# A graph layer on one core: batches of four steps, gathers tied to one put, 384-byte rows, and a changed readiness test

## The chip, the cores and the metric

The kernel runs on one core of one Trainium2 chip. The metric is device time in microseconds (us) of one execution. Three runs of the kernel before gave 18110.78, 18131.4 and 18134.8 us; their median is 18131.4 us. A further execution was recorded by the hardware profiler, and all rows of a profile come from it.

The engines are called as the profile calls them: PE is TensorE (its weight loads, which overlap the matmuls, are PEld), DVE is VectorE, ACT is ScalarE, POOL is GpSimd, and SP is SyncE, which issues most of the DMAs. L641 is line 641 of the kernel.

## The reference

A pre-norm graph layer over 100,000 nodes with 64 channels and 3,300,000 edges, sorted by the node that they end in (`dst`). In numpy terms:

```
h   = relu((x - mean(x)) / sqrt(var(x) + 1e-5))          # per node
y_e = concat(h[dst_e], h[src_e] - h[dst_e]) @ W.T + b    # per edge
s_v = sum of y_e over the edges with dst_e == v
out = x + where(cnt > 0, s / max(cnt, 1), 0)             # cnt: edges per node
```

The part of `y` that depends on `dst` is the same for all edges of a node, so only `h[src] @ W2.T`, 64 numbers a node, has to be summed over edges. The rest is one row a node.

## The kernel before, in words

**First stage.** In 28 iterations over the nodes, the kernel normalizes `x`, transposes it (`turned_of`), multiplies with the weights (`product`), and evicts the product in four parts (`evict`): the node's own part plus `x` plus bias goes to `hb` in float32 (`own`), and the part to be summed (`z`) is split into three bfloat16 numbers, high, middle and low (`first_part`, `second_part`, `third_part`), which together carry float32 precision. They are written to a table `h3` in HBM, one row a node: 3 x 64 numbers and two columns of ones, 388 bytes. The ones make each sum of rows bring its count of edges along. An order by hand (`turn`) fixes the sequence of instructions on each engine, in software-pipelined form: a new iteration is centred while the one before (`mid`) is transposed and multiplied and the one before that (`old`) is split.

**Two ways for the edges.** The sorted edges are cut into 256 windows of 8160 edges, which end in rows 0 to about 63,300, and a rest of 338 chunks of 28 x 128 edges.

- *Chunks.* For each 128 edges POOL issues an indirect DMA that gathers rows of `h3` (`chunks`, L641, 9464 of them) into one of 65 buffers `nb`; a burst of 28 matmuls (L606) against one-hot matrices (`hot_of`) sums a chunk by destination. ACT evicts it (L611), DVE adds the three parts, and SP adds it to its place in HBM (`addition`). `stored[1]` counts the chunks so written.
- *Windows.* First the edges of each window are sorted by source (DVE, with bitonic steps, L710 to L712). Then come the passes: 5 groups, each with one eighty-block share of the table held in SBUF (`tabs`), over 64 sets of four windows, 40 steps to a set. A step has a *pick* (`pick`, L1279: four matmuls that select rows of the table with one-hots `gh`, copied to `gs` by ACT at L1285) and a *put* (`put`, `by_quarters`, L1292: 16 matmuls on a quarter of the array's rows each, which add the picked rows to their destinations with one-hots `dh`). DVE makes the one-hots (`one_hots`, L1257 for `gh`, the helper `one_hot`, L553, for `dh` and for the chunks), in four parts for five steps. The four sums of a set fill four PSUM banks (`total`) and are evicted at its end (L1322, then DVE at L1326 and on). In the last group the sums are final, and SP writes them to HBM; `stored[0]` counts the windows.

**The order of the work in the passes.** `passes` runs over batches of three steps (`BATCH`; the first batch of a set has four): DVE's one-hots of later steps, at a set's start one burst of a chunk, the picks of the next batch, then the puts of this one. The picks use three PSUM banks in turn (`rings`); the eighth bank holds `pairs`, a copy of the ramp `upto` that L553 compares with.

The gathers are spread over the batches by `gathers`: each batch of steps adds its nominal time to `owed`, and for each 1270 ns owed one gather is issued, about 1.9 a batch. A gather is held back by a semaphore (`gated`): it waits for a mark, one of the picks or puts of the batch `BEHIND` = 6 back. The marks list has a batch's picks first and then its puts, and the gathers of a batch take marks spread evenly over the list (`at[i * len(at) // n]`).

**The results.** `results` makes the output in 98 blocks of 1024 rows: it loads two halves of the sums and `hb`, adds, divides by the count and adds again on DVE (L242 to L250), and stores. In the last three groups the passes call it once in two batches (`go_on`); what is left runs after the passes. The blocks are tried in an order that has the 35 blocks that only chunks reach first and then the window blocks from row 0 up. `ready` tells from the counts `stored` whether all that a block needs has been written:

```python
        left, now, before = list(order), None, []
        while left or now:
            before.append(tuple(stored))
            r = next((r for r in left if ready(r, before.pop(0) if len(before) > 2 else (0, 0))), None)
```

The counts grow as the instructions are written out, so this choice is made when the program is built. A result takes five calls: one that starts the loads, two that put DVE's work in place, one that waits and one that starts the store.

Of the kernel before, what the change touches and what calls it, by code (L numbers as in the profile page):

```python
# [13 lines left out]
F32 = mybir.dt.float32  # L14
# [20 lines left out]
NBUF = 65  # L35
# [4 lines left out]
BATCH = 3  # L40
# [8 lines left out]
BEHIND = 6  # L49
# [59 lines left out]
def gnn_preln(ctx: ExitStack, tc, x, src_w, dst_w, src_p, dst_p, src_a, dst_a, wT, b, out, V, E):  # L109
# [51 lines left out]
    h3 = dram.tile([RT, CT], BF16, name="h3")  # L161
# [67 lines left out]
    def results(pool, order, after, start):  # L229
# [27 lines left out]
        while left or now:  # L257
            before.append(tuple(stored))
            r = next((r for r in left if ready(r, before.pop(0) if len(before) > 2 else (0, 0))), None)
            coming = None  # L260
            if r is not None:
                left.remove(r)
                coming = load(r)
            yield
            if now:
                yield from finish(*now)
            else:
                yield
            now = coming
# [8 lines left out]
    with tc.tile_pool(name="pre", bufs=2) as pre, tc.tile_pool(name="small", bufs=4) as small, \  # L278
# [21 lines left out]
        blank = pre.tile([P, CT], BF16, name="blank", bufs=1)  # L300
# [118 lines left out]
        def first_part(i):  # L419

            own, z = owns_z[i]
            parts = split[i] = pre.tile([P, T, CT], BF16, name="parts", bufs=3)
            turn(nc.gpsimd.memset(parts[:, :, C3:], 1.0))
            turn(nc.scalar.copy(parts[:, :, :C], z))
            turn(nc.gpsimd.tensor_tensor(z, z, parts[:, :, :C], ALU.subtract))
# [17 lines left out]
        for i in range(-1, NT1 + 1):  # L443
# [8 lines left out]
            if has(old):  # L452
                evict(old, 3)
            if has(mid):
                turned_of(mid, 0)
            if has(old):
                first_part(old)
# [30 lines left out]
    with tc.tile_pool(name="rows", bufs=6) as rows, \  # L488
# [3 lines left out]
        pairs = rows_ps.tile([P, CH // 2], I32, name="pairs", bufs=1)  # L492
        nc.vector.tensor_copy(pairs, upto.bitcast(I32))
        upto = pairs.bitcast(I16)
# [29 lines left out]
        count = [0, 0]  # L524
        rings = [rows_ps.tile([P, 512], F32, name="ring0", bufs=1)]
# [34 lines left out]
        def chunks(first, n, dynamic=None):  # L560
# [68 lines left out]
            for e in range(n * J):  # L629
# [8 lines left out]
                if not in_passes[0]:  # L638
                    burst(20)
                nbs[e] = rows.tile([P, CT], BF16, name="nb", bufs=NBUF)  # L640
                last[POOL] = gated(nc.gpsimd.indirect_dma_start(  # L641
                    out=nbs[e], out_offset=None, in_=h3,
# [566 lines left out]
        def passes():  # L1209
# [5 lines left out]
            def fetch(t):  # L1215
# [17 lines left out]
                if final and s == 2 * SL + 1:  # L1233
                    owns[v] = load.tile([P, QW, NT, CT], BF16, name="own", bufs=1)
                    for r in range(QW):
                        at = number(wb_r[0:1, ds(u * QW + r, 1)], SP, V - CH)
                        sync(owns[v][:, r], h3[ds(at, CH)].rearrange("(b p) f -> p b f", p=P))
                if final and s == 2 * SL + 4:
                    beyond[v] = rows_x = load.tile([P, 1, CT], BF16, name="rows_x", bufs=2)
                    last[POOL] = nc.gpsimd.indirect_dma_start(  # L1240
                        out=rows_x[:, 0], out_offset=None, in_=h3,
                        in_offset=bass.IndirectOffsetOnAxis(ap=spilled[0][:, u:u + 1], axis=0))
# [25 lines left out]
            def pick(t):  # L1268
# [6 lines left out]
                gs[t] = hots.tile([P, 2, CE], BF16, name="gs", bufs=2 * BATCH + 1)  # L1275
# [85 lines left out]
            for of, ahead in zip(batches, batches[1:] + [()]):  # L1361
                for q in of:
                    fetch(q + AHEAD)
                    if q % SL < 2 * NT:
                        one_hots(q - q % SL + SL, q % SL)
# [15 lines left out]
        def load_table(k, g):  # L1381

            for i in range(2):
                sync(tabs[k][:, i],
# [3 lines left out]
        with tc.tile_pool(name="few", bufs=1) as few:  # L1388
# [3 lines left out]
            def gathers(ns):  # L1392
# [4 lines left out]
                for i in range(n):  # L1397
                    if at:
                        gate[0] = at[i * len(at) // n]
# [15 lines left out]
            with ExitStack() as held:  # L1415
                with tc.tile_pool(name="keys", bufs=1) as big, tc.tile_pool(name="counts", bufs=1) as counts:
# [6 lines left out]
                    rings.extend(g_ps.tile([P, 512], F32, name=f"ring{i}") for i in (1, 2))  # L1423
# [4 lines left out]
                with tc.tile_pool(name="load", bufs=3) as load, tc.tile_pool(name="hots", bufs=3) as hots, \  # L1428
                        tc.tile_pool(name="a_ps", bufs=1, space=PSUM) as a_ps:
                    for k in range(NBT):  # L1430
                        tabs.append(load.tile([P, 2, SL * NT, CT], BF16, name=f"tab{k}", bufs=1))
# [52 lines left out]
    with tc.tile_pool(name="any", bufs=2) as edge, tc.tile_pool(name="any_c", bufs=1) as one, \  # L1484
# [5 lines left out]
        with tc.For_i(0, n_slow, 1) as c:  # L1490
# [7 lines left out]
            nb = edge.tile([P, JA, CT], BF16, name="nb")  # L1498
            for j in range(JA):
                nc.gpsimd.indirect_dma_start(  # L1500
                    out=nb[:, j], out_offset=None, in_=h3,
# [85 lines left out]
```

## Time and profile before

| what | value |
|---|---|
| runs, median | 18131.4 us |
| the profiled execution's own time | 18148.31 us |
| its span in the trace | 18146.6 us |
| PE busy | 13049.6 us (72%) |
| DVE busy | 10919.6 us (60%) |
| POOL busy | 9972.4 us (55%) |
| ACT busy | 7142.4 us (39%) |
| passes, from and to | 2769 to 17867 us |
| what runs after the passes | 280 us |

The profiled execution is some 17 us above the median of the runs. A share of busy time is an average over the stages: in the first some 450 us the product of `x` is made, then the sort of the windows runs to about 2350 us with DVE in the lead, then the windows' borders are placed, and the passes take the most of the span. Rows of a timeline give start and length in us, the engine, line and operation, the count of instructions that the row joins, and in brackets the idle time of the engine before it with what ended it. "issue" is time in which the engine waited for nothing that the profile shows.

### The profile page before, as it was taken

How to read it: one execution, taken by the hardware profiler on the slowest of the kernel's cores; microseconds unless marked ns; L12 is line 12 of the kernel's file. 1: busy time of each engine (PE TensorE's matmuls, PEld its weight loads, DVE VectorE, ACT ScalarE, POOL GpSimd, SP SyncE). 2: the span in 40 equal slices, each digit the busy share in tenths (PEclk: the TensorE clock that was granted, in tenths of full speed). 3: DMA queues.
4: the chain of work that ended last, by engine and by line, in shares of the span. 5: the costliest groups of instructions: out<-in, count | busy, mean ns of one | idle time of the engine just before them, and what ended most of it. 6: DMA issues, size and time to landing. Idle time of an engine off the chain costs nothing. (4 is left out here: it accounts for less than half of the span.)

```text
span 18146.6 us, 617591 instructions
## 1 busy us (share of the span) xinstructions
PE 13049.6 (72%) x264285; PEld 10030.0 (55%) x264285; DVE 10919.6 (60%) x17830; ACT 7142.4 (39%) x15829; POOL 9972.4 (55%) x9922
## 2 busy tenths in 40 slices
PE   6111107888888888888888888888888888888883
PEld 4010105666666666666666666666666666666662
DVE  6788886666666654555555555555555555555555
ACT  5233353434444343344444444443444344444441
POOL 6666645555555555555555555555555555555551
PEclk8555558999999998999999999999999999999996
DMA  5511124333333433333444433343334345444446
GB/s 199 198 36 37 37 60 114 101 98 98 100 100 100 116 102 89 95 102 103 120 131 109 104 103 103 103 122 103 103 104 103 102 110 124 115 115 114 115 115 192
DMA packets 1630181, 1948.47 MB, mean 107 GB/s; under 512 B 998138, under 2 KB 1001794, under 8 KB 1622466
## 3 DMA queue, kind: packets, MB, share of 16 engines
q1 hardware_dynamic: 1307332, 1415.01, 27.2%
q0 software_dynamic: 316480, 493.19, 12.8%
q8 instruction: 2066, 33.85, 0.8%
q14 instruction: 703, 5.76, 0.1%
q10 hardware_dynamic: 3600, 0.67, 0.0%
HBM read 1626.63 MB, written 281.14 MB: 105 GB/s over the span
## 5 line engine op out<-in xcount | busy, mean ns | idle before, releaser
L641 POOL DMA_INDIRECT nb<-h,si x9464 | 9342.2, 987 | 7297.4 <-PE ring L1279 3969.3
L1285 ACT CAST gs<-ring 128x386 bf16<-128x386 f32 x12800 | 5386.9, 491 | 8015.4 <-PE ring L1279 7411.6
L1292 PE MATMUL total<-gs,dh 32*128 32x193 bf16 x200704 | 6803.3, 249 | 2029.7 <-issue 1784.1
L1292 PEld LDWEIGHTS <-dh 32*128 32x128 bf16 x200704 | 4578.6, 94 | 4096.0 <-issue 3902.7
L553 DVE TENSOR_TENSOR dh<-dt,pairs 128x1536 bf16<-128x1536 int16 (+1 forms) x5120 | 3998.2, 816 | 4257.0 <-PE total L1292 2461.5
L1279 PE MATMUL ring<-tab,gh 128*128 128x193 bf16 x50176 | 5278.3, 252 | 572.0 <-issue 206.7
L1279 PEld LDWEIGHTS <-gh 128*128 128x128 bf16 x51200 | 4228.9, 99 | 1303.9 <-issue 850.4
L1257 DVE TENSOR_SCALAR gh<-srs,who_f 128x1280 bf16<-128x1280 int16 x5120 | 2698.0, 566 | 2072.9 <-PE ring L1279 1843.6
L606 PE MATMUL ring<-nb,hot 128*128 128x193 bf16 x9464 | 1016.4, 271 | 1830.2 <-issue 865.0
L606 PEld LDWEIGHTS <-hot 128*128 128x128 bf16 x9464 | 886.4, 107 | 1941.3 <-issue 1022.3
L710 ACT COPY tmp<-keys 128x1536 f32<-128x1536 f32 (+26 forms) x525 | 647.6, 1243 | 895.4 <-DVE keys L712 434.0
L711 DVE TENSOR_TENSOR keys<-tmp,keys 128x1536 f32<-128x1536 f32 (+26 forms) x525 | 749.6, 1459 | 333.5 <-issue 185.5
L553 DVE TENSOR_TENSOR hot<-near,pairs 128x896 bf16<-128x896 int16 x1352 | 780.6, 611 | 0.0
L712 DVE TENSOR_TENSOR keys<-tmp,keys 128x1536 f32<-128x1536 f32 (+26 forms) x525 | 750.2, 1455 | 0.9
L1322 ACT COPY whole<-total 128x386 f32<-128x386 f32 x1280 | 522.6, 496 | 468.4 <-PE total L1292 344.9
L1326 DVE TENSOR_TENSOR whole<-whole 128x512 f32<-128x512 f32 x640 | 439.7, 687 | 29.6 <-ACT whole L1322 13.0
L611 ACT COPY stage<-ring 128x193 f32<-128x193 f32 x338 | 109.1, 323 | 727.9 <-remote 418.3
L1165 DVE COPY_PREDICATED kw<-bits,kw 128x504 int32<-128x504 int32 (+11 forms) x637 | 328.4, 516 | 17.1
L396 PE MATMUL o_ps<-weights,hT 128*128 128x256 f32 x784 | 246.5, 466 | 120.9 <-ACT hT L388 84.7
L1140 POOL DMA_INDIRECT kw<-ksort,at x196 | 195.0, 995 | 245.2 <-DVE bits L1161 75.1
L396 PEld LDWEIGHTS o_ps<-weights,hT 128*128 128x128 f32 x784 | 173.0, 233 | 170.8 <-ACT hT L388 91.5
L616 DVE TENSOR_REDUCE sums<-stage 128x64 f32<-128x192 f32 x338 | 124.0, 367 | 180.5 <-ACT stage L611 109.2
(196 smaller groups left out, 3128.8 us busy)
## 6 DMA issues: line engine op xcount, KB each, us to landing
srs<-sr_d SPq DMA_DIRECT2D x2560, 320.0 KB
nb<-h,si POOLq DMA_INDIRECT x9464
part_d<-wsums SPq DMA_DIRECT2D x256, 260.0 KB
prev<-part_d SPq DMA_DIRECT2D x256, 260.0 KB
acc<-zeros SPq DMA_DIRECT2D x56, 910.0 KB
dt<-dt_d SPq DMA_DIRECT2D x2560, 10.0 KB
tab<-h SPq DMA_DIRECT2D x80, 485.0 KB
h<-parts SPq DMA_DIRECT2D x28, 1358.0 KB
```

Of the source, the lines that this page charges most:

```text
L553: return nc.vector.tensor_tensor(out.rearrange("p k (a d) -> p k a d", d=D), numbers[:, :, None].to_broadcast(shape), upto[:shape[0], :n]. ...
L606: in_turn(nc.tensor.matmul(ps[:, :CE], lhsT=hots_of[q, j // JH][:, j % JH], rhs=nbs.pop(q * J + j)[:, :CE], start=j == 0, stop=j == J - 1))
L641: last[POOL] = gated(nc.gpsimd.indirect_dma_start(out=nbs[e], out_offset=None, in_=h3, in_offset=bass.IndirectOffsetOnAxis(ap=of[q][1][:, ...
L710: last[ACT] = nc.scalar.copy(tmp, lo)
L711: nc.vector.tensor_tensor(lo, tmp, hi, ALU.min)
L712: last[DVE] = nc.vector.tensor_tensor(hi, tmp, hi, ALU.max)
L1257: nc.vector.tensor_scalar(ghots[v, k][:, part].rearrange("p c i s -> p (c i s)"), srs[v, k].rearrange("p c i s -> p (c i s)"), who_f[:, pa ...
L1279: mm = nc.tensor.matmul(gp[:, i], lhsT=ghots[v, k][:, b, c, i], rhs=of[:, :CE], start=b == 0, stop=b == NT - 1)
L1285: in_turn(nc.scalar.copy(gs[t], gp))
L1292: mm = nc.tensor.matmul(total[:, r, b * CE:b * CE + CE], lhsT=dh[at, i, b * P:b * P + P], rhs=rows_of[at, i, :CE], start=begin and i == 0 ...
L1322: in_turn(nc.scalar.copy(whole[:, r], total[:, r, :NT * CE]))
L1326: todo.append(lambda i=i: nc.vector.tensor_add(summed[:, :, :C], summed[:, :, :C], whole[:, :, i * C:i * C + C]))
```

## The change

The change has five parts.

1. Batches of four steps in place of three (`BATCH`), ten to a set. `gs` has eight buffers, the rings get a fourth PSUM bank, and the copy `pairs` goes away: L553 reads `upto` from SBUF. The four parts of the one-hots are made at steps 0, 1, 3 and 4 of five.
2. All gathers of a batch wait for the same mark, the put ahead of the last one of the batch four back.
3. The rows of `h3` have 384 bytes, without the two columns of ones. The ones are written once into the buffers that the rows are loaded to (`with_ones`): 63 fixed buffers for the gathers, the eight tables, `own` and `rows_x`; the memset of each iteration's `parts` goes away.
4. In the first stage `evict(old, 3)` comes after `turned_of(mid, 0)`.
5. In `results` the counts are taken from `before` once for a call and used for all blocks that are tried.

```diff
-NBUF = 65
+NBUF = 63
-BATCH = 3
+BATCH = 4
+PARTS_AT = 0, 1, 3, 4
-BEHIND = 6
+BEHIND = 4
...
-    h3 = dram.tile([RT, CT], BF16, name="h3")
+    h3 = dram.tile([RT, C3], BF16, name="h3")
...
             before.append(tuple(stored))
-            r = next((r for r in left if ready(r, before.pop(0) if len(before) > 2 else (0, 0))), None)
+            then = before.pop(0) if len(before) > 2 else (0, 0)
+            r = next((r for r in left if ready(r, then)), None)
...
-            parts = split[i] = pre.tile([P, T, CT], BF16, name="parts", bufs=3)
-            turn(nc.gpsimd.memset(parts[:, :, C3:], 1.0))
+            parts = split[i] = pre.tile([P, T, C3], BF16, name="parts", bufs=3)
...
-            if has(old):
-                evict(old, 3)
             if has(mid):
                 turned_of(mid, 0)
             if has(old):
+                evict(old, 3)
                 first_part(old)
...
-        pairs = rows_ps.tile([P, CH // 2], I32, name="pairs", bufs=1)
-        nc.vector.tensor_copy(pairs, upto.bitcast(I32))
-        upto = pairs.bitcast(I16)
...
+        def with_ones(pool, shape, name):
+            rows_of = pool.tile([P, *shape, CT], BF16, name=name, bufs=1)
+            axes = " ".join("abc"[:len(shape)])
+            flat = rows_of.rearrange(f"p {axes} f -> p ({axes}) f") if shape else rows_of[:, None]
+            nc.vector.memset(flat[:, :, C3:], 1.0)
+            return rows_of
+
+        fetched_rows = [with_ones(rows, (), f"nb{i}") for i in range(NBUF)]
...
-                nbs[e] = rows.tile([P, CT], BF16, name="nb", bufs=NBUF)
+                nbs[e] = fetched_rows[e % NBUF]
                 last[POOL] = gated(nc.gpsimd.indirect_dma_start(
-                    out=nbs[e], out_offset=None, in_=h3,
+                    out=nbs[e][:, :C3], out_offset=None, in_=h3,
...
-                gs[t] = hots.tile([P, 2, CE], BF16, name="gs", bufs=2 * BATCH + 1)
+                gs[t] = hots.tile([P, 2, CE], BF16, name="gs", bufs=2 * BATCH)
...
-                    if q % SL < 2 * NT:
-                        one_hots(q - q % SL + SL, q % SL)
+                    if q % SL in PARTS_AT:
+                        one_hots(q - q % SL + SL, PARTS_AT.index(q % SL))
...
                     if at:
-                        gate[0] = at[i * len(at) // n]
+                        gate[0] = at[max(0, len(at) - 2)]
...
-                    rings.extend(g_ps.tile([P, 512], F32, name=f"ring{i}") for i in (1, 2))
+                    rings.extend(g_ps.tile([P, 512], F32, name=f"ring{i}") for i in (1, 2, 3))
...
-                        tabs.append(load.tile([P, 2, SL * NT, CT], BF16, name=f"tab{k}", bufs=1))
+                        tabs.append(with_ones(load, (2, SL * NT), f"tab{k}"))
+                    own_rows = with_ones(load, (QW, NT), "own")
+                    spilled_rows = [with_ones(load, (1,), f"rows_x{i}") for i in range(2)]
```

The loads of the tables, of `own` and of `rows_x` write only the first 192 columns in the same way.

More of the change, by code (lines that the diff above doesn't have):

```diff
@@ L299, in gnn_preln @@
         load_x(T)
-        blank = pre.tile([P, CT], BF16, name="blank", bufs=1)
+        blank = pre.tile([P, C3], BF16, name="blank", bufs=1)
         nc.gpsimd.memset(blank, 0.0)
@@ L1233, in fetch @@
                 if final and s == 2 * SL + 1:
-                    owns[v] = load.tile([P, QW, NT, CT], BF16, name="own", bufs=1)
+                    owns[v] = own_rows
                     for r in range(QW):
                         at = number(wb_r[0:1, ds(u * QW + r, 1)], SP, V - CH)
-                        sync(owns[v][:, r], h3[ds(at, CH)].rearrange("(b p) f -> p b f", p=P))
+                        sync(owns[v][:, r, :, :C3], h3[ds(at, CH)].rearrange("(b p) f -> p b f", p=P))
                 if final and s == 2 * SL + 4:
-                    beyond[v] = rows_x = load.tile([P, 1, CT], BF16, name="rows_x", bufs=2)
+                    beyond[v] = rows_x = spilled_rows[v % 2]
                     last[POOL] = nc.gpsimd.indirect_dma_start(
-                        out=rows_x[:, 0], out_offset=None, in_=h3,
+                        out=rows_x[:, 0, :C3], out_offset=None, in_=h3,
                         in_offset=bass.IndirectOffsetOnAxis(ap=spilled[0][:, u:u + 1], axis=0))
@@ L1383, in load_table @@
             for i in range(2):
-                sync(tabs[k][:, i],
+                sync(tabs[k][:, i, :, :C3],
                                   h3[ds((i * NCB + g * SG + k * SL) * CELL, SL * CELL)].rearrange("(x p) f -> p x f", p=P))
@@ L1498, in gnn_preln @@
             nb = edge.tile([P, JA, CT], BF16, name="nb")
+            nc.vector.memset(nb[:, :, C3:], 1.0)
             for j in range(JA):
                 nc.gpsimd.indirect_dma_start(
-                    out=nb[:, j], out_offset=None, in_=h3,
+                    out=nb[:, j, :C3], out_offset=None, in_=h3,
                     in_offset=bass.IndirectOffsetOnAxis(ap=si[:, j:j + 1], axis=0))
```

## The prediction

> **What bounds the kernel now.** I read the page first (busy shares, the granted clock, the groups), then windows, then timelines of single batches.
>
> ```profile
> span 18146.6 us, 617591 instructions
> PE 13049.6 (72%) x264285; PEld 10030.0 (55%) x264285; DVE 10919.6 (60%) x17830; ACT 7142.4 (39%) x15829; POOL 9972.4 (55%) x9922
> L641 POOL DMA_INDIRECT nb<-h,si x9464 | 9342.2, 987 | 7297.4 <-PE ring L1279 3969.3
> L1292 PE MATMUL total<-gs,dh 32*128 32x193 bf16 x200704 | 6803.3, 249 | 2029.7 <-issue 1784.1
> ```
>
> No engine is full. In the passes TensorE leads, and its largest idle is 1784.1 us in the puts (L1292) where no engine is named as the cause. The windows that follow are two groups of the passes, with the gathers alone counted (columns: length, POOL busy and count, granted clock, DMA share, GB/s):
>
> ```profile
> 9038.00:12014.00 2976.00, 1624.96 (x1641) 0.98 0.42 111
> 14990.00:17867.00 2877.00, 1531.67 (x1541) 0.98 0.48 115
> ```
>
> A group is 64 sets, so the first is 2976 / 64 = 46.5 us a set; the clock is nearly full, and the DMA share is under a half. Now a batch of three steps without any gather, at the very end of the passes:
>
> ```profile
> 17847.11 1.19 PE L1279 MATMUL ring<-tab,gh 128*128 128x193 bf16 x12
> 17848.23 1.19 PE L1292 MATMUL total<-gs,dh 32*128 32x193 bf16 x48
> ```
>
> Picks take 1.12 us, puts as much: 2.24 us a batch. A usual batch holds two gathers, apart:
>
> ```profile
> 12003.86 1.18 PE L1279 MATMUL ring<-tab,gh 128*128 128x193 bf16 x12
> 12004.98 1.53 PE L1292 MATMUL total<-gs,dh 32*128 32x193 bf16 x43
> 12006.95 0.32 PE L1292 MATMUL total<-gs,dh 32*128 32x193 bf16 x5 [0.45 <-issue]
> 12007.21 1.02 PE L1279 MATMUL ring<-tab,gh 128*128 128x193 bf16 x10
> 12003.91 0.94 POOL L641 DMA_INDIRECT nb<-h,si  x1 [0.67 <-PE total L1292]
> 12005.63 1.14 POOL L641 DMA_INDIRECT nb<-h,si  x1 [0.78 <-PE ring L1279]
> ```
>
> It takes 12007.21 − 12003.86 = 3.35 us, 1.1 more. The first gather, started with the picks, let TensorE run on through the picks; the second, started in the puts, is followed by TensorE standing in them. So I read it thus: while a gather is issued, and some tenths after, TensorE gets only so far ahead (here some 40 matmuls), then stands. **The passes are bound by TensorE plus these holds**, the tail by results that come after the passes.
>
> **The change part by part.** All against the profiled execution's span, 18146.6 us.
>
> *Readiness test (the tail).* Rows: the last additions of the results (L250; count, the shortest, median and longest duration in ns, first and last start), asked of the tail, and the last matmul, which waited 272.38 us.
>
> ```profile
> L250 DVE TENSOR_TENSOR ht<-ht,at x63: 691/691/693, 17881.9 to 18133.0; 128x512 f32<-128x512 f32 x63
> 18138.85 0.37 PE L1533 MATMUL f_ps<-ident,fewest 128*1 128x128 f32 x1 [272.38 <-DVE fewest L1531]
> ```
>
> 63 of 98 blocks end after the passes, (18133.0 − 17881.9) / 62 = 4.05 us each. The code says why: in `results` the pop from `before` stands inside the search, so only the first block of `left` meets the true counts; the others meet (0, 0) and are never ready. That first block is one that waits for chunks until near the end, though the window blocks behind it are long ready. With one `then` for all they go in the last group. A result takes five calls, the passes call once in two batches, ten batches a set: one result a set, 64 in the group. A chunk covers 3584 × 100000 / 3.3 million = 108.6 rows, a block of 1024 rows takes 9.4 chunks, and at one burst a set about 7 of the 64 turns go to such blocks. A window block needs 1024 / 247 = 4.1 windows, and 4 windows end per set, so these keep step, two or three sets late. About 54 of 63 leave the tail: −54 × 4.05 = **−219 us**. The last group and the tail by windows (PE, PEld, DVE, ACT, POOL busy):
>
> ```profile
> 14990.00:17867.00 2877.00, 2423.93 (x50220) 1884.12 (x50217) 1590.80 (x2707) 1190.01 (x2871) 1590.18 (x1603) 0.98 0.48 115
> 17867.00:18147.00 280.00, 0.37 (x1) 0.08 (x1) 162.97 (x447) 1.16 (x4) 0.00 (x0) 0.51 0.76 241
> ```
>
> A result costs DVE 162.97 / 63 = 2.6 us. In the last group DVE is 1590.80 of 2877 busy, which covers 54 × 2.6 = 140 us. Uncovered it would cost the 140. On SP's queue each brings three loads and a store among the fetches of `srs` and `dt`, which run ten steps (some 12 us) ahead; the true counts are those of two turns before, so a load seldom waits there for the additions that it reads. A result moves 128 × 8 × (65 + 65 + 64 + 64) × 4 bytes = 1.06 MB, 54 of them 57 MB or 20 GB/s beside the group's 115. Bounds −250 to −80.
>
> *First stage.* ACT's copies in one iteration, and the product's wait in two:
>
> ```profile
> 215.91 0.37 ACT L408 COPY z<-o_ps 128x256 f32<-128x256 f32 x1 [1.67 <-DVE own L406]
> 216.18 0.59 ACT L388 COPY hT<-t_ps 128x512 f32<-128x512 f32 x1
> 216.83 3.68 PE L396 MATMUL o_ps<-weights,hT 128*128 128x256 f32 x8 [2.66 <-ACT hT L388]
> 231.92 0.79 PE L396 MATMUL o_ps<-weights,hT 128*128 128x256 f32 x1 [2.66 <-ACT hT L388]
> ```
>
> Iterations take 231.92 − 216.83 = 15.09 us, and TensorE waits 2.66 in each for the hT copy, which stands on ACT behind the last z copy, itself 1.67 us late. `evict(old, 3)` moved behind the first transposes puts the hT copy ahead, 1.67 us earlier at most. The z copy gets later by 0.59, and `first_part`'s cast and POOL's subtraction with it; these end well ahead of their next use. I take 1.5 × 27 = **−40 us**; bounds −45 to 0.
>
> *Ones once.* 28 memsets leave POOL's side of the first stage (nothing waits); 74 small ones come on DVE, 63 of them in the sort, where DVE is the bound. The nearest row, 128x1 copies with their median of 140 ns:
>
> ```profile
> L618 DVE COPY sums<-stage x338: 132/140/152, 571.6 to 17833.2; 128x1 f32<-128x1 f32 x169
> ```
>
> 63 × 0.14 = **+9 us**, bounds 0 to 10. The 384-byte rows, two buffers fewer, the gate's distance (four batches of four are 16 steps, six of three were 18) and the parts' new places I take at 0: the DMA share is 0.42, and of all waits of TensorE, the bursts' for gathered rows come to little (columns: total, times, longest), which bounds these edits at ±63 us:
>
> ```profile
> PE ring L606 <- DMA nb<-h,si: 63.3, 37, 10.6
> ```
>
> *Four steps a batch.* Inside a run matmuls follow at (1.19 − 0.25) / 11 = 0.085 us; twelve are 1.03, yet the next kind starts after 1.12: 0.09 a switch, 0.18 a batch. (The Trainium skill, "TensorEngine Tiling (Array Packing)", Key Properties, has it that changing the tiling mode drains TensorE first; the trace agrees, with these 0.09 us.) A set of 40 steps had 13 batches and now has 10: 3 × 0.18 × 320 = −173 us; some of it lies under holds, **−160**, bounds −175 to −50.
>
> *The gathers' gate.* Both or all three gathers of a batch now wait for one mark, the put ahead of the last in the batch four back, so they start together, back to back. Behind a waiting gather POOL's queue holds only gathers, and the bursts that want their rows come 28 or more gathers later. Two such cases lie in the old trace by chance; two together:
>
> ```profile
> 16285.89 1.19 PE L1279 MATMUL ring<-tab,gh 128*128 128x193 bf16 x12
> 16289.32 0.85 PE L1279 MATMUL ring<-tab,gh 128*128 128x193 bf16 x8
> 16286.09 0.94 POOL L641 DMA_INDIRECT nb<-h,si  x1 [0.98 <-PE total L1292]
> 16287.33 0.94 POOL L641 DMA_INDIRECT nb<-h,si  x1 [0.30 <-issue]
> ```
>
> 3.43 − 2.24 = 1.2 us held. Three together:
>
> ```profile
> 7641.16 1.19 PE L1279 MATMUL ring<-tab,gh 128*128 128x193 bf16 x12
> 7645.80 0.93 PE L1279 MATMUL ring<-tab,gh 128*128 128x193 bf16 x9
> 7641.18 0.94 POOL L641 DMA_INDIRECT nb<-h,si  x1 [3.03 <-PE total L1292]
> 7643.67 0.94 POOL L641 DMA_INDIRECT nb<-h,si  x1 [0.30 <-issue]
> ```
>
> 4.64 − 2.24 = 2.4 held. A batch of four is 2.24 + 8 × 0.085 = 2.92, and what TensorE runs ahead covers 0.25 to 0.3 more of each hold: 0.95 and 2.1. The group's 1641 gathers over 640 batches are 2.56 a batch: 4.4 batches of a set hold two, 5.6 three: 4.2 + 11.8 = 16.0 us a set, less 1.6 where a burst at the set's start fills the hold: 14.4. Before, 46.5 a set less 13 × 2.24, one step more (0.7) and the burst's 28 matmuls (2.4) leaves 14.3. So **0**. Bounds: if a gather holds only one piece of 0.45, as in the usual batch's row, 2.56 × 10 × 0.45 = 11.5 a set, −2.8 × 320 = −900; if TensorE runs no further ahead than before, 4.4 × 1.2 + 5.6 × 2.4 − 1.6 = 17.1 a set, +2.8, +900. I take 0, as the two rows give it.
>
> *`upto` from SBUF.* L553 read it from PSUM; now both its inputs lie in SBUF. Gathers over L553, and over an operation on SBUF alone (L1257):
>
> ```profile
> 17708.45 1.55 DVE L553 TENSOR_TENSOR dh<-dt,pairs 128x1536 bf16<-128x1536 int16 x2 [0.19 <-PE total L1292]
> 17708.69 0.94 POOL L641 DMA_INDIRECT nb<-h,si  x1 [0.73 <-PE total L1292]
> 17720.25 1.01 DVE L1257 TENSOR_SCALAR gh<-srs,who_f 128x1280 bf16<-128x1280 int16 x2
> 17720.34 1.27 POOL L641 DMA_INDIRECT nb<-h,si  x1 [0.74 <-PE ring L1279]
> ```
>
> 0.94 beside 1.27, up to 0.33 us more. A set has eight such pairs of L553, 1.55 in every 46.5 / 8 = 5.8 us, a quarter of the time, so up to a third of some 8000 gathers (1600 a group) meet it: 0 (no price) to 8000 × 0.33 × 0.33 = 870, as the hold passes it on. Single gathers' length was not passed on (the 1.14 above left 3.35), back-to-back spacing is: I take a sixth, **+150**. (The Trainium skill, "GPSIMD Engine Reference", says that GpSimd shares its SBUF path with VectorE and meets it where VectorE has two SBUF inputs: it speaks against this edit, and the 0.94 beside 1.27 agrees.)
>
> *Fourth ring bank.* It can take some of the picks' wait for casts (columns as above): **−30**, bounds −190 to 0.
>
> ```profile
> PE ring L1279 <- ACT gs L1285: 188.6, 204, 1.9
> ```
>
> Sum: −219 − 40 + 9 − 160 + 0 + 150 − 30 = −290. 18146.6 − 290 = 17,857 for an execution like the profiled one, whose own time is 18148.31. The median of the runs is 18131.4, 17 lower: **17,840 us**.
>
> **The rivals.** *A, slower: the holds drop the clock.* Three windows around a triple (PE, PEld, DVE, ACT, POOL busy; granted clock, DMA share, GB/s):
>
> ```profile
> 10728.00:10731.40 3.40, 2.98 (x84) 2.26 (x72) 3.40 (x8) 1.78 (x4) 2.05 (x3) 1.00 0.39 117
> 10731.40:10734.80 3.40, 2.40 (x26) 1.83 (x27) 0.91 (x2) 0.00 (x1) 2.20 (x2) 0.80 0.40 101
> 10734.80:10738.20 3.40, 3.40 (x64) 2.71 (x62) 2.53 (x4) 1.32 (x4) 2.04 (x2) 0.70 0.22 62
> ```
>
> TensorE issued 26 matmuls in 3.40 us, the clock fell, and the next 3.40 us were full and brought only 64 (84 in 2.98 us at the granted 1.00 before). Usually holds come in pieces of 0.45; in 5.6 triples a set, each lengthened by contention, they gather in one window. It decides where some 5% of batches do so: a window at half clock loses at most 1.7 us, less what a hold would have taken anyway, say 1.3; at one batch in ten that is 320 × 1.3 = +420. With contention at 450 instead of 150, +300: 17,840 + 720 = 18,560, and 18,350 with half the drops. (The Trainium skill, "TensorE: Matmul & The Clock Gate", Part 1, has the clock halve after an idle window; the trace agrees with 0.80 and 0.70.) Against it: the groups keep 0.98 though every usual batch is held 1.1. Price 18,450; chance 0.30, of which 0.26 slower, 0.04 near none.
>
> *B, faster: the hold costs less.* Only one mark a batch is now to be passed on in time, so TensorE may run further past gathers. Triples held 1.9 us instead of 2.1 make 4.2 + 10.6 − 1.6 = 13.2 a set, −1.2 × 320 = −380: 17,460; at the lower bound, −900, 16,940. For it: a gather begun with the picks cost nothing at 12003.91. Against: the triple's 2.4. Chance 0.24.
>
> *C: the readiness test doesn't do what it says*, as when the results can't keep pace: the tail keeps 280 us, 17,840 + 219 = 18,059. For it: one result a set leaves no slack. Chance 0.08.
>
> **How the numbers follow.** Forecast 0.38, A 0.30, B 0.24, C 0.08. Time 17,840, the forecast's. The forecast's own range is 17,700 to 18,000 (tail, switches and contention by half). The whole goes from 17,300, below B's price, to 18,500, above A's; about a third of B and two fifths of A lie outside, 0.2. What can be told from no change is about 0.2%, 18,095 to 18,168. Faster: 0.38 + 0.24 + 0.08 − 0.04 (C or the forecast ending near none) = 0.66; same 0.04 + 0.04 = 0.08; slower 0.26.
>
> **What would show it.** Tail: fewer than 12 of L250 after the passes' end, the tail 60 us or so. First stage: iterations of 13.5 us. Switches: ten batches a set, 2.92 where no gather is. Gate: gathers in twos and threes 1.24 us apart; sets near 46.2 us in the middle groups. Contention: L641's mean above 987 ns, over 1.05. Clock: the middle groups' 0.98 kept; 0.9 or less means A. A middle group over 3100 us would make the prediction wrong on the slow side, under 2800 on the fast side.

## The result, and the profile after

The changed kernel takes 17,977.04 us in the median (17,966.12 to 17,990.65), the kernel before 18,131.47: a ratio of 0.9918 with a 95% interval of 0.99 to 0.9935, or 154 us less. Forecast were 17,840 us, or 291 less. The range held the time and the sign was right; about half of the gain is missing, and the terms of the sum that came out otherwise are larger than that: they partly cancel. Two of the executions behind the numbers further down, one of the kernel before (18,550.45 us) and one of a variant of it (18,532.56 us), ran at a granted clock of 0.72 and 0.69 in place of some 0.89; without them the ratio 0.986 given there is 0.987.

Rows of the changed kernel's page (L647 is the gather that was L641, L1298 the put that was L1292):

```profile
L647 POOL DMA_INDIRECT nb<-h,si x9464 | 10239.9, 1082 | 6605.8 <-PE total L1298 4050.9
L1298 PE MATMUL total<-gs,dh 32*128 32x193 bf16 x200704 | 6518.7, 253 | 2403.1 <-issue 2328.0
```

The gathers' mean rose from 987 to 1082 ns, so they do meet the one-hots that now read SBUF, and the puts' idle time without a named cause rose from 1784.1 to 2328.0 us. The same windows as before, a middle group, the last one and the tail, with the gathers alone counted (length, POOL busy and count, granted clock, DMA share, GB/s):

```profile
8929.00:11928.00 2999.00, 1799.04 (x1642) 0.94 0.41 110
14921.00:17917.00 2996.00, 1690.16 (x1545) 0.92 0.51 128
17917.00:17989.00 72.00, 0.00 (x0) 0.53 0.55 171
```

The tail went from 280 to 72 us. The middle group takes 2999 us in place of 2976, and the last 2996 in place of 2877; the clock in them went from 0.98 to 0.94 and 0.92. The last additions of the results in the tail (count, durations in ns, first and last start), and the first stage with the transition from one iteration's product to the next:

```profile
L251 DVE TENSOR_TENSOR ht<-ht,at x11: 691/691/694, 17931.5 to 17975.8; 128x512 f32<-128x512 f32 x11
214.14 1.99 PE L398 MATMUL o_ps<-weights,hT 128*128 128x256 f32 x8 [0.61 <-ACT hT L390]
226.64 1.99 PE L398 MATMUL o_ps<-weights,hT 128*128 128x256 f32 x8 [0.61 <-ACT hT L390]
```

Eleven results are left in the tail in place of 63. An iteration of the first stage takes 226.64 − 214.14 = 12.50 us in place of 15.09.

What holds TensorE in the passes is seen in two batches of four steps:

```profile
10505.06 1.52 PE L1285 MATMUL ring<-tab,gh 128*128 128x193 bf16 x16
10506.52 0.99 PE L1298 MATMUL total<-gs,dh 32*128 32x193 bf16 x31
10507.96 0.28 PE L1298 MATMUL total<-gs,dh 32*128 32x193 bf16 x4 [0.45 <-issue]
10508.69 0.32 PE L1298 MATMUL total<-gs,dh 32*128 32x193 bf16 x5 [0.45 <-issue]
10509.43 0.71 PE L1298 MATMUL total<-gs,dh 32*128 32x193 bf16 x24 [0.42 <-issue]
10510.08 2.47 PE L1285 MATMUL ring<-tab,gh 128*128 128x193 bf16 x16
10512.49 2.15 PE L1298 MATMUL total<-gs,dh 32*128 32x193 bf16 x64
10505.12 0.94 POOL L647 DMA_INDIRECT nb<-h,si  x1 [0.81 <-PE total L1298]
10506.36 1.11 POOL L647 DMA_INDIRECT nb<-h,si  x1 [0.30 <-issue]
10507.78 1.11 POOL L647 DMA_INDIRECT nb<-h,si  x1 [0.30 <-issue]
```

Three gathers start with the picks at 10505.06 and follow each other; the batch takes 10510.08 − 10505.06 = 5.02 us, 2.10 more than the 2.92 without gathers, and that is the price that was forecast for a triple (three gathers in one batch). The next batch shows the second price: its 16 picks take 10512.49 − 10510.08 = 2.41 us, where the batch ahead took 1.46. That is the half clock: the granted clock is 1.00 over the held batch and 0.57 over these picks, though no pause in the held batch is longer than 0.45 us.

### The profile page after: what moved, and what is told of

It is laid out like the page before. It is cut to its first block, busy times and chain, and to the rows that moved or that the text cites. A ratio compares the mean times of both kernels' runs of the same rounds, so it can differ in the third digit from the quotient of the medians.

```text
span 17988.8 us, 612045 instructions
## 1 busy us (share of the span) xinstructions
PE 12952.3 (72%) x264285; PEld 10417.8 (58%) x264285; DVE 11051.6 (61%) x17903; ACT 7448.8 (41%) x15829; POOL 10887.5 (61%) x9894
## 5 line engine op out<-in xcount | busy, mean ns | idle before, releaser
L647 POOL DMA_INDIRECT nb<-h,si x9464 | 10239.9, 1082 | 6605.8 <-PE total L1298 4050.9
L1291 ACT CAST gs<-ring 128x386 bf16<-128x386 f32 x12800 | 5706.3, 489 | 7489.3 <-PE ring L1285 6205.0
L1298 PE MATMUL total<-gs,dh 32*128 32x193 bf16 x200704 | 6518.7, 253 | 2403.1 <-issue 2328.0
L1298 PEld LDWEIGHTS <-dh 32*128 32x128 bf16 x200704 | 4670.1, 96 | 4078.1 <-issue 3868.4
L559 DVE TENSOR_TENSOR dh<-dt,upto 128x1536 bf16<-128x1536 int16 (+1 forms) x5120 | 4014.7, 822 | 3658.8 <-PE total L1298 2386.3
L1285 PE MATMUL ring<-tab,gh 128*128 128x193 bf16 x50176 | 5398.4, 263 | 397.7 <-ACT stage L617 213.9
L1285 PEld LDWEIGHTS <-gh 128*128 128x128 bf16 x51200 | 4569.0, 103 | 1056.8 <-issue 860.5
L1263 DVE TENSOR_SCALAR gh<-srs,who_f 128x1280 bf16<-128x1280 int16 x5120 | 2747.7, 577 | 2399.4 <-PE ring L1285 2094.6
L559 DVE TENSOR_TENSOR hot<-near,upto 128x896 bf16<-128x896 int16 x1352 | 786.3, 619 | 0.0
L398 PE MATMUL o_ps<-weights,hT 128*128 128x256 f32 x784 | 206.5, 406 | 96.6 <-ACT hT L390 68.6
```

Source lines behind the costliest of these rows:

```text
L559: return nc.vector.tensor_tensor(out.rearrange("p k (a d) -> p k a d", d=D), numbers[:, :, None].to_broadcast(shape), upto[:shape[0], :n]. ...
L647: last[POOL] = gated(nc.gpsimd.indirect_dma_start(out=nbs[e][:, :C3], out_offset=None, in_=h3, in_offset=bass.IndirectOffsetOnAxis(ap=of[q ...
L1263: nc.vector.tensor_scalar(ghots[v, k][:, part].rearrange("p c i s -> p (c i s)"), srs[v, k].rearrange("p c i s -> p (c i s)"), who_f[:, pa ...
L1285: mm = nc.tensor.matmul(gp[:, i], lhsT=ghots[v, k][:, b, c, i], rhs=of[:, :CE], start=b == 0, stop=b == NT - 1)
L1291: in_turn(nc.scalar.copy(gs[t], gp))
L1298: mm = nc.tensor.matmul(total[:, r, b * CE:b * CE + CE], lhsT=dh[at, i, b * P:b * P + P], rhs=rows_of[at, i, :CE], start=begin and i == 0 ...
```

## The experiments

The runs were made in four sittings, A to D, and these differ. In A the kernel before takes 18,125.37 us, close to the 18,131.47 of the result above, whose chip isn't on record; in B it takes 13,787.64, in C 18,378.66 and in D 18,385.77. Each comparison is with the kernel before in the same sitting. The record numbers the chips of the sittings 12, 6, 6 and 11: B and C bear the same number, 25 minutes apart, and the record doesn't say whether that is one chip at two times or two chips. So what differs between the sittings need not be the chip. No trace of the kernel before was kept in A to D; rows of it are those of the profile before.

### One part of the change alone (sitting A)

**The readiness test.**

```diff
-            r = next((r for r in left if ready(r, before.pop(0) if len(before) > 2 else (0, 0))), None)
+            then = before.pop(0) if len(before) > 2 else (0, 0)
+            r = next((r for r in left if ready(r, then)), None)
```

> The kernel before with the readiness test of the change alone. The changed kernel's tail fell from 280 to 72 us, but its last group took 120 us more than before. By the prediction's sum the results cost nothing under the passes: the time falls by the tail alone, about 205 us, and the last group stays at 2877 us. The rival: the results that move into the last group take back time there whatever the gathers do, some 1.5 us a set, about 100 us: the time falls by only 100 to 120 us, and the last group takes some 2975 us. A third reading: the 120 us in the last group are the clock's doing (its share of half speed went from 3% to 15%) and come with back-to-back gathers, not with the results: then the last group here is within 30 us of 2877.

17,912.74 us, ratio 0.9882 (0.9866 to 0.9899): 213 us less. Its last group (PE, PEld, DVE, ACT, POOL busy; clock, DMA share, GB/s):

```profile
14970.00:17844.00 2874.00, 2420.31 (x50211) 1875.86 (x50209) 1711.59 (x3099) 1188.65 (x2869) 1599.56 (x1603) 0.99 0.57 136
```

What runs after the passes takes 59 us. DVE's busy time in the last group rose from 1590.80 to 1711.59 us, and the group stayed at 2874 (2877 before), with the clock at 0.99. The results' work under the passes costs nothing that these runs can tell. The rival that they take back 100 us falls.

**The first stage's order.**

```diff
-            if has(old):
-                evict(old, 3)
             if has(mid):
                 turned_of(mid, 0)
             if has(old):
+                evict(old, 3)
                 first_part(old)
```

> The kernel before with the first stage's order of the change alone (the memsets of ones are kept). In the changed kernel an iteration of the first stage takes 12.50 us in place of 15.09, 70 us in all, where 40 were predicted. If the order alone does it, by the wait of 2.66 us that also let the clock fall in each iteration: 68 to 72 us less. If the rest came with the memsets that left POOL: 40 to 45 us less and iterations of 13.5 us.

18,054.45 us, ratio 0.9958 (0.9941 to 0.9975): 71 us less, all of what the changed kernel gains there. The products of two iterations, and then the first stage by windows (same columns as above), of the kernel before and of this one:

```profile
217.17 1.99 PE L396 MATMUL o_ps<-weights,hT 128*128 128x256 f32 x8 [0.61 <-ACT hT L388]
229.67 1.99 PE L396 MATMUL o_ps<-weights,hT 128*128 128x256 f32 x8 [0.61 <-ACT hT L388]
```

```profile
100.00:400.00 300.00, 210.40 (x833) 159.62 (x831) 208.89 (x198) 174.80 (x236) 216.39 (x79) 0.84 0.58 205
```

```profile
100.00:380.00 280.00, 199.11 (x945) 148.98 (x945) 235.03 (x225) 198.99 (x270) 246.30 (x90) 1.00 0.71 251
```

The order alone makes the iteration 12.50 us. The granted clock goes from 0.84 to 1.00: before, the eight matmuls that followed the wait of 2.66 us took 3.68 us (the row at 216.83), now they take 1.99. So the wait cost 1.7 us behind itself, in slow matmuls. The wait itself fell by 2.66 − 0.61 = 2.05 us, and a new one of 1.32 us ahead of the next eight matmuls took a part back. (The Trainium skill, "TensorE: Matmul & The Clock Gate", section "Why this matters for your kernels", advises no idle gaps over some 3 us between bursts of matmuls, or the clock halves. Here the longest gap of an iteration was 2.66 us and the clock 0.84; with none over 1.32 us it is 1.00.)

**The ramp `upto` from SBUF.**

```diff
-        pairs = rows_ps.tile([P, CH // 2], I32, name="pairs", bufs=1)
-        nc.vector.tensor_copy(pairs, upto.bitcast(I32))
-        upto = pairs.bitcast(I16)
```

> The kernel before with the one-hots' ramp read from SBUF alone (no copy in PSUM, the rings keep three banks). The gathers' mean should rise from 987 to about 1070 ns in each theory. If their length is passed on as the prediction took it, a sixth of the worst case: 100 to 200 us slower. If a lone gather's length does not reach TensorE, since the hold of a lone gather did not depend on its length: within 30 us of before, with the clock at 0.97 or above in the middle groups.

18,092.44 us, ratio 0.998 (0.997 to 0.9989): 33 us less, though the gathers' mean rose to 1125 ns. The page's row of the gathers, and a middle group with them alone:

```profile
L638 POOL DMA_INDIRECT nb<-h,si x9464 | 10644.8, 1125 | 5953.8 <-PE ring L1276 2631.9
9017.00:11988.00 2971.00, 1895.65 (x1641) 0.96 0.45 111
```

POOL's busy time in the group went from 1624.96 to 1895.65 us, the clock from 0.98 to 0.96, and yet the group is 5 us shorter. Longer gathers are not passed on to TensorE here, and a somewhat lower clock alone doesn't make a group longer. The time lies just past the 30 us of the second expectation, on the fast side, and the clock just under its 0.97. Why the kernel gains was not tried.

### The mark undone (sitting A)

```diff
-                        gate[0] = at[max(0, len(at) - 2)]
+                        gate[0] = at[i * len(at) // n]
```

> The changed kernel with the gathers of a batch tied to marks spread over the batch four back, as before, in place of one mark. By the prediction's sum two or three gathers together hold TensorE as long as the same number apart: within 60 us of the changed kernel. By the clock's reading, the long holds of gathers back to back are what lets the clock fall (12% of the middle groups at half speed, 4 to 5% before): spread, the clock goes back to 0.97, and at about 0.56 us a gather a set of ten batches takes 2.92 x 10 + 25.6 x 0.56 + 2.4 = 46.0 us in place of 46.8, some 200 to 280 us less than the changed kernel. The other side: with more gathers started in the puts the holds grow, and the time rises by over 100 us.

17,653.08 us, ratio 0.974 (0.9723 to 0.9756): 324 us less than the changed kernel's 17,977.04, more than any of the expectations named, and faster than both kernels. A middle group and the last one, with the gathers alone:

```profile
8813.00:11758.00 2945.00, 1882.06 (x1642) 0.96 0.44 112
14704.00:17552.00 2848.00, 1791.27 (x1543) 0.97 0.56 135
```

A set of the middle group takes 2945 / 64 = 46.0 us. The clock came back from 0.94 to 0.96. The middle group is 2999 − 2945 = 54 us shorter than in the changed kernel, and the last one 148 us, with the same results in it. The one mark costs some 324 us, and nearly half of that lies in the last group.

### Where gathers hold nothing (sitting B)

Four variants of the changed kernel: the ramp back in PSUM with three banks for the rings; the readiness test undone; and the one mark moved to the first put, and to the first pick.

```diff
+        pairs = rows_ps.tile([P, CH // 2], I32, name="pairs", bufs=1)
+        nc.vector.tensor_copy(pairs, upto.bitcast(I32))
+        upto = pairs.bitcast(I16)
...
-                    rings.extend(g_ps.tile([P, 512], F32, name=f"ring{i}") for i in (1, 2, 3))
+                    rings.extend(g_ps.tile([P, 512], F32, name=f"ring{i}") for i in (1, 2))
```

> The changed kernel with the one-hots' ramp back in PSUM and three banks for the rings. The gathers' mean should fall from 1082 to about 1000 ns. If, with gathers back to back, their length is passed on to TensorE (the prediction's +150, which did not show where gathers are apart: there the ramp in SBUF alone made the kernel 33 us faster): 100 to 250 us faster than the changed kernel, and the half-speed share of the middle groups falls from 12% to 6 to 8%. If it is not passed on here either, the lost bank and the 33 us count: 20 to 80 us slower than the changed kernel.

13,886.03 us, ratio 1.0075 (1.0058 to 1.0092).

```diff
-            then = before.pop(0) if len(before) > 2 else (0, 0)
-            r = next((r for r in left if ready(r, then)), None)
+            r = next((r for r in left if ready(r, before.pop(0) if len(before) > 2 else (0, 0))), None)
```

> The changed kernel without the readiness test. The tail comes back, about 208 us. With the gathers spread, the results in the last group cost nothing (alone on the kernel before they took 2875 us for that group against 2877). If they do cost with gathers back to back, the last group falls from 2996 to about 2900 us and the time rises by only 110 us, to 18,085. If the gate alone sets the last group's time: it stays within 25 us of 2996 and the time is about 18,185.

14,888.99 us, ratio 1.08 (1.0782 to 1.0818).

```diff
-                        gate[0] = at[max(0, len(at) - 2)]
+                        gate[0] = at[max(0, len(at) - 4)]
```

> The changed kernel with all gathers of a batch tied to the first put of the batch four back in place of the put ahead of the last: they still go back to back, some 0.7 us earlier in the batch. If what costs is that they go together, the time stays within 80 us of the changed kernel. If what costs is where in the batch they begin (spread, most begin in the last puts ahead of the picks, and a pair begun there holds TensorE 0.55 us, a pair begun with the picks 0.7 to 1.1): about 200 us faster than the changed kernel.

14,769.57 us, ratio 1.0717 (1.0699 to 1.0735).

```diff
-                        gate[0] = at[max(0, len(at) - 2)]
+                        gate[0] = at[0]
```

> The changed kernel with all gathers of a batch tied to the first pick of the batch four back: back to back, some 0.6 us later against the steps than in the changed kernel. If what costs is that they go together: within 80 us of the changed kernel. If what costs is where in the batch they begin, a pair begun well inside the picks holds TensorE 1.2 to 1.7 us and the time is 150 us or more above the changed kernel.

14,761.65 us, ratio 1.071 (1.0692 to 1.0728).

All four expectations took the holds for granted, and this sitting does not show them. Batches of the last of the four, with gathers running all the time:

```profile
8503.46 1.52 PE L1285 MATMUL ring<-tab,gh 128*128 128x193 bf16 x16
8504.92 1.52 PE L1298 MATMUL total<-gs,dh 32*128 32x193 bf16 x64
8506.37 1.52 PE L1285 MATMUL ring<-tab,gh 128*128 128x193 bf16 x16
8502.75 0.94 POOL L647 DMA_INDIRECT nb<-h,si  x1 [0.30 <-issue]
8503.99 1.16 POOL L647 DMA_INDIRECT nb<-h,si  x1 [0.30 <-issue]
8505.46 0.94 POOL L647 DMA_INDIRECT nb<-h,si  x1 [0.30 <-PE total L1298]
```

The batch takes 2.91 us, the time without gathers. In the whole run the puts stand 21.6 us without a named cause, where the changed kernel's stood 2328.0. POOL has work all the time. A middle group of this kernel, with the gathers alone, and then one of the kernel with the ramp in PSUM:

```profile
7432.00:9801.00 2369.00, 1868.07 (x1631) 0.93 0.54 139
7119.00:9244.00 2125.00, 1617.66 (x1633) 0.99 0.61 155
```

With the 0.30 us of issue ahead of each gather, the gathers fill 1868.07 + 1631 × 0.30 = 2357 of 2369 us, and 1617.66 + 1633 × 0.30 = 2108 of 2125. So POOL is the bound in these groups.

The gathers' length then sets the time, and the place of the mark does not (14,770 beside 14,762): the ramp in SBUF, with the fourth bank, costs 14,762 − 13,886 = 876 us there. That is near the full worst case of the prediction, 870, but not by its reckoning: the gathers of the whole kernel got longer by 10606.5 − 9343.6 = 1263 us, more than the prediction allowed for, and a part of that stayed hidden. The two kernels with another mark differ from the changed kernel in nothing else, so by an estimate the change would be some 7% slower there; the changed kernel itself wasn't run in this sitting.

The readiness test, undone, costs 14,889 less some 14,766 = 123 us there, less than its 213 in sitting A. The traces show where the rest went: with the results in it the last group takes 2483 us (the kernel with the mark at the first pick), without them 2396, 87 us less. With them TensorE waits 284 us in that group for DVE's one-hots, without them 63. So where TensorE isn't held, DVE's work for the results is no longer covered.

### The mark with the ramp in PSUM (sitting C)

> The changed kernel with the one-hots' ramp back in PSUM and three banks for the rings, once more, for a chip on which gathers hold TensorE (the kernel before at 18,130 us). If, with gathers back to back, their length is passed on to TensorE: 100 to 250 us faster than the changed kernel's 17,977, with the half-speed share of the middle groups down from 12% to 6 to 8%. If not, the lost bank and the 33 us of the ramp alone count: 20 to 80 us slower, some 18,030. On a chip where gathers hold nothing (the kernel before at 13,790 us) it should repeat 13,886.

18,524.98 us, ratio 1.0083 (1.0066 to 1.01). The same with spread marks (both edits shown above together):

> The changed kernel with spread marks, the ramp back in PSUM, and three banks for the rings. Where gathers hold TensorE: if the ramp in SBUF costs nothing with gathers apart, 20 to 80 us slower than with spread marks alone (17,653 us), some 17,700; if batches of four steps pass the gathers' length on, 50 to 150 us faster, some 17,550. Where they hold nothing, POOL is the bound and only the gathers' length counts, not their marks: within 100 us of 13,886.

17,741.97 us, ratio 0.9656 (0.964 to 0.9672). These two stand in one sitting and differ in the mark alone: it costs 783 us. A middle group and the last one, with the gathers alone, with the one mark and then spread:

```profile
9138.00:12244.00 3106.00, 1595.95 (x1643) 0.93 0.41 106
15344.00:18446.00 3102.00, 1509.10 (x1545) 0.94 0.51 124
```

```profile
8886.00:11843.00 2957.00, 1633.44 (x1642) 0.98 0.44 112
14790.00:17664.00 2874.00, 1535.32 (x1543) 0.99 0.55 134
```

With the one mark the last group, which has some 100 gathers fewer, is as long as the middle one; spread, it is 83 us shorter. Three gathers in a batch and the start of the batches behind it, with the one mark and then spread:

```profile
10121.79 1.71 PE L1288 MATMUL ring<-tab,gh 128*128 128x193 bf16 x16
10126.86 1.71 PE L1288 MATMUL ring<-tab,gh 128*128 128x193 bf16 x16
10130.61 1.71 PE L1288 MATMUL ring<-tab,gh 128*128 128x193 bf16 x16
10121.80 0.95 POOL L650 DMA_INDIRECT nb<-h,si  x1 [1.53 <-PE total L1301]
10123.05 1.07 POOL L650 DMA_INDIRECT nb<-h,si  x1 [0.30 <-issue]
10124.42 0.95 POOL L650 DMA_INDIRECT nb<-h,si  x1 [0.30 <-issue]
```

```profile
10058.39 1.19 PE L1288 MATMUL ring<-tab,gh 128*128 128x193 bf16 x12
10060.32 0.50 PE L1288 MATMUL ring<-tab,gh 128*128 128x193 bf16 x4 [0.74 <-ACT gs L1294]
10062.20 1.31 PE L1288 MATMUL ring<-tab,gh 128*128 128x193 bf16 x12
10066.92 1.19 PE L1288 MATMUL ring<-tab,gh 128*128 128x193 bf16 x12
10058.25 0.95 POOL L650 DMA_INDIRECT nb<-h,si  x1 [0.63 <-PE total L1301]
10059.96 0.95 POOL L650 DMA_INDIRECT nb<-h,si  x1 [0.77 <-PE ring L1288]
10061.66 0.95 POOL L650 DMA_INDIRECT nb<-h,si  x1 [0.75 <-PE total L1301]
```

Together, 1.25 to 1.37 us from start to start, the batch takes 10126.86 − 10121.79 = 5.07 us. Spread, 1.7 us from start to start, the batch takes 10062.20 − 10058.39 = 3.81, in spite of a wait for a cast that the missing fourth bank brings. But this is not the whole price: the third spread gather, begun at 10061.66, still runs when the next batch begins. The batch behind, with two more gathers, takes 10130.61 − 10126.86 = 3.75 us with the one mark, and 10066.92 − 10062.20 = 4.72 spread. Over both batches, with five gathers, it is 8.82 beside 8.53 us. If every two batches went like these, that would be, as an estimate, 0.29 × 1600 = 464 of the 783 us (5 groups of 64 sets of ten batches); the rest these rows do not explain, but the middle group's clock is 0.93 with the one mark and 0.98 spread.

What the ramp in PSUM does with the one mark can't be told across sittings: this ratio, 1.0083, belongs to C, and 0.9918 to a sitting like A.

### The mark with three steps, and the mark moved (sitting D)

```diff
-                        gate[0] = at[i * len(at) // n]
+                        gate[0] = at[max(0, len(at) - 2)]
```

(on the kernel before, with its batches of three)

> The kernel before (batches of three) with the one mark alone: all gathers of a batch tied to the put ahead of the last in the batch six back. Where gathers hold TensorE: by the rows of the prediction a pair together takes 3.43 to 3.5 us a batch, apart 3.32, thirteen batches a set: 1.5 to 2.3 us a set, 480 to 700 us slower than before. If the mark's cost in the changed kernel (324 us by spreading it) came only with four steps and triples, pairs of three-step batches cost nothing: within 60 us of before. Where gathers hold nothing (the kernel before at 13,790 us): within 60 us of before in both.

18,156.18 us, ratio 0.986 (0.9792 to 0.9928): 230 us **less** than the kernel before. Both expectations miss. Two batches with one gather and two, and the last two groups with the gathers alone:

```profile
10026.31 1.18 PE L1279 MATMUL ring<-tab,gh 128*128 128x193 bf16 x12
10028.55 1.19 PE L1279 MATMUL ring<-tab,gh 128*128 128x193 bf16 x12
10031.90 1.19 PE L1279 MATMUL ring<-tab,gh 128*128 128x193 bf16 x12
10026.41 0.95 POOL L641 DMA_INDIRECT nb<-h,si  x1 [1.17 <-PE total L1292]
10028.57 0.95 POOL L641 DMA_INDIRECT nb<-h,si  x1 [1.21 <-PE total L1292]
10029.82 1.24 POOL L641 DMA_INDIRECT nb<-h,si  x1 [0.30 <-issue]
```

```profile
8994.00:11963.00 2969.00, 1611.38 (x1643) 0.98 0.44 111
14911.00:17870.00 2959.00, 1507.20 (x1543) 0.98 0.49 112
```

One gather begun with the picks holds nothing (10028.55 − 10026.31 = 2.24 us, a batch without gathers); two hold 3.35 − 2.24 = 1.1 us. With 1643 gathers over 64 x 13 batches, 1.97 a batch, most are pairs; four-step batches have 2.56, and so many triples. The clock stays at 0.98. The pair's 3.35 us is what two gathers apart took in the prediction's row, so these rows don't show where the 230 us come from, and the kernel before has no trace from this sitting. A mark that goes with a gain in batches of three (sitting D) and with a loss in batches of four (A and C) is no fault of the mark alone: by these runs the two edits act on each other. That the triples are what makes the difference is argued, not shown.

> The changed kernel with the one mark moved to the first put of the batch four back, once more, for a chip on which gathers hold TensorE (the changed kernel there at 0.992 of the kernel before, with spread marks 0.974). If what costs is that gathers go together: 0.988 to 0.996 of the kernel before. If what costs is where in the batch they begin: 0.976 to 0.982.

18,609.58 us, ratio 1.0102 (1.0048 to 1.0157), outside both ranges: they were made from the ratios of sitting A, which do not hold here. The nearest kernel with the mark in its old place is the one of sitting C (ratio 1.0083, a middle group of 3106 us, as here), and it has the ramp in PSUM and three banks. So nothing shows that moving the mark ahead helps, and whether the place in the batch counts stays open: the changed kernel itself has no time in this sitting.

## Why the prediction was right or wrong

The terms beside what the runs of sitting A gave:

| term of the sum | forecast, us | measured, us |
|---|---|---|
| readiness test | −219 | −213, alone |
| first stage | −40 | −71, alone |
| ramp from SBUF | +150 | −33, alone |
| four steps, fourth bank, ones (−160 − 30 + 9) | −181 | −156, as the rest of the spread kernel's −472, if the parts add up |
| one mark | 0 | +324, by undoing it |

The last two rows are worked out from the kernel with spread marks, so it is no check of the terms that they add up to −149 beside the measured −154.

- **Readiness test: right**, in its size and in that DVE's spare time covers the results (1711.59 of 2874 us busy). Eleven results were left, where nine were counted. Rival C falls. In sitting B, where TensorE wasn't held, it was worth only 123 us.
- **First stage: the mechanism right, the size wrong, beyond its bound of −45.** The sum took off the ACT copy's 1.67 us of waiting, at most; the wait of TensorE fell by 2.05. Above all it left out what the wait did to the clock, though the prediction's own row shows it: eight matmuls in 3.68 us behind the wait.
- **Ramp from SBUF: the contention came, its price did not.** The gathers' mean rose past the forecast 1.05 us where the ramp alone was moved (1125 ns), and the kernel was 33 us faster. The step that failed is "I take a sixth": where gathers have gaps, a longer gather only fills them. Where POOL has none (sitting B), it cost up to 876 us, with the fourth bank in it.
- **Four steps: right within the uncertainty of a remainder.** They were not run apart from the bank and the memsets; the passes begin 77 us earlier (2692 in place of 2769) and 71 of them are the first stage's, so the memsets cost nothing seen.
- **One mark: the step that failed.** The price of a triple was good: 2.1 us were forecast and 2.10 measured in the row shown. But the sum set "16.0 less 1.6" against the 14.3 of the kernel before and stopped there. Left out was, first, the half clock behind the holds, which it had as rival A: the middle groups fell to 0.94, between the 0.98 of the forecast and the 0.9 named for A, so A came in a small dose. (The prediction's window ahead of the drop was not idle, it held 26 matmuls, and the held batch ahead of the half clock shown above had all its 80.) A middle set took 2999 / 64 = 46.9 us, less 29.2 of work and 2.4 of burst leaves 15.3, not 14.4. Second, the last group: its 100 gathers fewer shorten it by 99 us in the kernel before (2976 to 2877), and by 97 with spread marks (2945 to 2848), but with one mark it is as long as its neighbour (2996 beside 2999). In sitting C it is the same (2957 to 2874 spread, 3106 and 3102 with one mark), and nearly so with three steps and no results in it (2969 and 2959). That this is the mark's doing is shown by A and C; why fewer gathers bring nothing there stays open. How the 324 us divide between slow clock and longer holds was not isolated either: with the ramp alone moved the clock fell to 0.96 at no cost.

The passes as a whole were forecast to take 40 us less and took 127 more (2692 to 17,917, or 15,225, in place of 15,098), a difference of 167 us. The last group has 128 of these: it got 120 us longer, where 8 less were forecast.

## What to carry to other kernels

Price a wait on TensorE with the clock that follows it: the row behind the wait, not the wait alone, tells the gain of removing it. When two edits change how many things fall together (longer batches, and one mark for all of a batch), cost them as a pair, against the same longer batches without the mark; in batches of three the mark went with a gain of 230 us, in batches of four it gave up 324. A contention costs what the lengthened engine has no gaps for, so look first whether that engine is the bound. Ask of a gather's price over two batches, not one, since what starts late in a batch is paid for in the next. And where a hold of unknown cause sets the time, measure in more than one sitting, the kernel before each time.

## What the runs showed of the hardware

The hold itself, which adds to the time of the passes in three of four sittings, is not there in the fourth: the same kernel before takes 13,788 us in place of 18,125 to 18,386, batches with gathers running take their bare 2.91 us, and POOL becomes the bound of the middle groups. What makes the hold, and what differs between the sittings, no run here tells; two of them, one with the hold and one without, bear the same chip number.

With holds, spreading the gathers helps in batches of four (324 and 783 us), but by less than one batch shows: a batch with three gathers 1.25 to 1.37 us from start to start took 5.07 us and one with three at 1.7 us only 3.81, yet with the batch behind it, five gathers in all, it was 8.82 beside 8.53. In batches of three, two gathers took 3.35 us at 1.25 us from start to start and at 1.7. A lone gather begun with the picks held nothing.

(The Trainium skill, "GPSIMD Engine Reference", Specifications, names the shared SBUF interfaces as a place of contention with VectorE. The trace agrees in the gathers' means, 987 and 1125 ns; whether that costs time differed between the sittings, from −33 us where TensorE was held to some +876 where POOL was the bound, the latter with the fourth bank in it.)
